# Graph stage: the centre's share in spare rows, layer two's outputs turned by VectorE, and layer one's mapped products in fp32 instead of three bf16 parts

## The chip, the core and the metric

The kernel runs on one core of one Trainium2 chip. Its engines have a queue of instructions each and work beside one another: TensorE (PE, with its weight loads shown apart as PEld), VectorE (DVE), ScalarE (ACT), GpSimd (POOL) and SyncE (SP), which here only starts DMAs. Semaphores tie them together. The metric is device time in microseconds; lower is better. About 0.2% is what a measurement of this kernel can tell from no change.

## What is computed

One layer of a model in three parts: a cross-attention that is a graph convolution over 512 nodes, a state-space scan, and a feed-forward part. The change is in the first. There are 16 batches, 512 nodes each, 32 channels; for each of 4 orders (two Morton, two Hilbert, from the coordinates) a node has K = 10 neighbours, a window of its place in the order.

```python
def _get_graph_features(feats, inds_list, perm, W_lin, b_lin, k=10):
    for inds in inds_list:                       # 4 orders
        neigh = gather(feats, inds)              # (B, N, k, C)
        gf = concat([broadcast(center), neigh - center], -1)
    ...
    x16 = x.astype(float16).astype(float32)      # (B*N, k, 256): 8 heads of 32
    scores = einsum('bihd,bjhd->bhij', qh, qh) / sqrt(32)
    attn = softmax(scores, -1)                   # k x k for each head and node
    out = einsum('bhij,bjhd->bihd', attn, qh).reshape(B * N, k, 256)
    return out @ W_lin.T + b_lin                 # 64 channels

g1 = _get_graph_features(f0, inds_list, perm1, W_lin1, b_lin1)
h1 = lrelu(instance_norm(einsum('oc,bnkc->bonk', W_conv1, g1), (2, 3)))
feats1 = h1.max(-1)                              # 32 channels
g2 = _get_graph_features(feats1, inds_list, perm2, W_lin2, b_lin2)
h2 = lrelu(instance_norm(einsum('oc,bnkc->bonk', W_conv2, g2), (2, 3)))
feats2 = h2.max(-1)                              # 64 channels
h3 = einsum('oc,bcn->bon', W_conv3, concat([feats, feats1, feats2], 1))
return lrelu(instance_norm(h3, (2,)))
```

The centre's half of the heads has the same row ten times, so attention leaves it as it is: its share of an output is a linear map of the node's own features plus the bias, the same for the node's ten rows.

## The kernel before

`graph_part` first makes the sort keys of the nodes (`node_orders`, VectorE, integer operations), then ranks by comparing all keys (L556, L557), then works through eight passes, `order`: four groups of four batches, each through layer one (32 output channels, `co`) and later layer two (64; `npair` is 1 and 2): (0,1), (1,1), (0,2), (2,1), (1,2), (3,1), (2,2), (3,2) as group and layer. The instruction order is written out by hand (`manual_schedule`): each engine gets its instructions in the order of the program. Before the passes GpSimd writes zeros into the tiles that need them (L437), DD and EN last.

A pass is 43 blocks of 12 nodes, 120 (node, neighbour) columns. A block's steps, in the loop at L1090, with how many blocks later each comes:

- `differences` (six blocks ahead): GpSimd subtracts the centre from the window, into DD (f16); every third block four DMAs on SP's queue copy DD into DX, ordered by head.
- `scores` (0): TensorE, a mask matmul (L862) and 16 matmuls (L869) of 120 columns. `greatest` (0): VectorE's maximum (L878). `expo` (1): a matmul subtracts it (L886), ScalarE takes the exponent (L891). `sums` and `shares` (1): VectorE sums (L898) and takes reciprocals (L904), GpSimd multiplies into EN (L906). `turn` (3): VectorE transposes EN in 32x32 blocks (L912) into e.
- `mapped` (0): TensorE takes the differences through the combined weights WA, which are kept as three bf16 parts: 4 x 3 x 4 = 48 matmuls (L931) of 4 `co` columns, each with 32 columns of DD as weights, so that four run beside one another in the array ("128*32"). ScalarE copies the result to `us` (L936).
- `outputs` (3): 16 fp32 matmuls (L959), `us` as weights and e as moving data, 30 columns each; layer one has 32-wide weights, layer two 64-wide ("128*64"). The profile shows each fp32 matmul as two. Columns are output channels' rows: channels lie on partitions. In layer one a matmul with the identity (L949) first writes the centre's share `hc`, repeated ten times, over four blocks' columns. In layer two VectorE adds `hc` (L976).
- `reduce` (4) and `rest` (5): VectorE takes the maximum over the neighbours (L982) and the moments (L985), every four blocks in layer one, every two in layer two.

Beside the blocks run, one piece a block, the preparation of the next pass (`prep`: transposes, one-hot rows by rank L767, placing matmuls L721, DMAs on SP's queue, and `share`, which makes `hc` with L682 and L683), the end of the last pass (`end`, `lrelu_norm`, `finish`) and the rank comparisons that are still wanted. e has 32 rows per block of three nodes, of which 30 are used.

Of the kernel before, what the change touches and what calls it, by code (L numbers as in the profile page):

```python
# [8 lines left out]
F32 = mybir.dt.float32  # L9
# [384 lines left out]
def graph_part(nc, tc, cx, I, dram, id32, ones, xt, F0, layernorm_steps, rstd_steps, scan_input):  # L394
# [43 lines left out]

    layers = []
    for L, co in ((1, 32), (2, 64)):  # L440
        WA = [gc.tile([P, 4, 4, co], BF16, name=f"WA{L}_{k}") for k in range(3)]
        WC = gc.tile([P, co // 32, P], F32, name=f"WC{L}")
        for t in (*WA, WC):
            zero(t)
        layers.append((L, co, co // 32, WA, WC, gc.tile([P, 1], F32, name=f"HB{L}")))

    KS = []
    for k in range(2):
# [14 lines left out]
    nc.vector.memset(W3, 0.0)  # L463
    for b in range(4):
        cols = slice(32 * b, 32 * b + 32)
        for j in range(2):
            nc.sync.dma_start(out=W3[cols, j, cols], in_=I["wc3T"][32 * j:32 * j + 32])
        nc.sync.dma_start(out=W3[64 * (b % 2):64 * (b % 2) + 64, 2 + b // 2, cols], in_=I["wc3T"][64:128])

    it2 = gc.tile([P, D], F16, name="it2")  # L470
    nc.gpsimd.iota(it2, pattern=[[2, D]], base=-(D - 1), channel_multiplier=0, allow_small_or_imprecise_dtypes=True)
# [18 lines left out]
        )  # L490
    for t in (*DD, *EN):
        zero(t)

    idb = gc.tile([P, P], BF16, name="idb")
    nc.scalar.copy(idb, id32)
# [4 lines left out]

    def weights(L, co, npair, WA, WC, HB):
        wa, wc, wt, bl = (loaded[n, L] for n in ("wlA", "wlC", "wcT", "bl"))


        pw = kps.tile([P, 4, co], F32, tag="w", name=f"pw{L}", bufs=2)
        for b in range(4):
            for h in range(4):
                nc.tensor.matmul(
                    pw[32 * b:32 * b + 32, h], lhsT=wa[:, 32 * h:32 * h + 32], rhs=wt, start=(h == 0), stop=True,
                    skip_group_check=True,  # L510
                )

        pc = kps.tile([P, co], F32, tag="w", name=f"pc{L}", bufs=2)
        for b in range(4):
            for m in range(M):
                nc.tensor.matmul(
                    pc[32 * b:32 * b + 32, :], lhsT=wc[:, 32 * m:32 * m + 32], rhs=wt,
                    start=(m == 0), stop=(m == M - 1),
                )
        yield  # L520
        rows = [slice(32 * b, 32 * b + 32) for b in range(4)]
        for k in range(3):
            for b, rb in enumerate(rows):
                nc.scalar.copy(WA[k][rb, :, b], pw[rb])
            if k == 2:
                break
            for b, rb in enumerate(rows):
                nc.tensor.matmul(
                    pw[rb], lhsT=nid[rb, rb], rhs=WA[k][rb, :, b], start=False, stop=True,
                    skip_group_check=True,  # L530
                )
        for b in range(4):
            pr, k = divmod(b * co, P)
            nc.scalar.copy(WC[32 * b:32 * b + 32, pr, k:k + co], pc[32 * b:32 * b + 32, :])

        wt4 = wp.tile([64, P], F32, name=f"wtr{L}")
        nc.scalar.copy(
            wt4.rearrange("p (r o) -> p r o", o=co), wt.unsqueeze(1).to_broadcast([64, P // co, co])
        )
        pb = kps.tile([P, 1], F32, tag="w", name=f"pb{L}", bufs=2)  # L540
        nc.tensor.matmul(pb, lhsT=wt4, rhs=bl, start=True, stop=True)
        nc.scalar.copy(HB, pb)


    sgn = keep.tile([P, D], BF16, name="sgn")
# [97 lines left out]
    def prep(g, layer, early=False):  # L643
# [26 lines left out]
        def share():  # L670

            c16 = wk.tile([P, D], F16, tag="c16", name=f"c16{key}", bufs=1)
            nc.vector.tensor_copy(c16, src)
            yield
            c32 = wk.tile([P, D], F32, tag="c32", name=f"c32{key}", bufs=1)
            nc.vector.tensor_copy(c32, c16)
            yield
            yield
            hc = wk.tile([P, npair, D], F32, tag="hc", name=f"hc{key}")
            for pr in range(npair):  # L680
                ph = ps_1.tile([P, D], F32, tag="misc", bufs=2, name=f"ph{key}_{pr}")
                nc.tensor.matmul(ph, lhsT=WC[:, pr], rhs=c32, start=True, stop=True)  # L682
                nc.scalar.activation(hc[:, pr], ph, AF.Identity, bias=HB)  # L683
                yield
            made[key][2] = hc

        made[key] = [None, None, None]
        if not at_hand:
# [154 lines left out]
    def begin(at):  # L843
        g, layer = order[at]
        L, co, npair, WA, WC, HB = layers[layer]
        key = keys[at]
        per = 4 // npair
        nst = -(-NGRP // per)
        mxo = wk.tile([P, npair, D], F32, tag="mxo", name=f"mxo{key}")
        stats = wk.tile([P, npair, nst, 6], F32, tag="stats", name=f"stats{key}")  # L850
        state[at] = key, co, npair, WA, made[key][2], per, mxo, stats

    def at_piece(at, gi):
# [54 lines left out]
    def turn(at, gi):  # L908
# [3 lines left out]
        nc.vector.transpose(e.rearrange("p i q -> p (i q)"), en.rearrange("p i q -> p (i q)"))  # L912
        live["e2", at, gi] = e

    def mapped(at, gi):

        key, co, npair, WA = state[at][:4]
        slot, c1 = at_piece(at, gi)
        d = DD[slot]
        us = sm.tile([P, NJ, 4 * co], F32, tag="us", name=f"us{at}_{gi}", bufs=4)  # L920
        u = None
        nj = NJ // npair
        for j in range(NJ):
            c0 = c1 + j * QB
            jj = j % nj
            if jj == 0:
                u = ps_2.tile([P, nj, 4 * co], F32, tag="u", name=f"u{at}_{gi}_{j}")
            for k in range(3):
                for h in range(4):
                    rh = slice(32 * h, 32 * h + 32)  # L930
                    nc.tensor.matmul(  # L931
                        u[rh, jj], lhsT=d[:, h, c0:c0 + 32], rhs=WA[k][:, h].rearrange("p b o -> p (b o)"),
                        start=(jj == 0 and k == 0), stop=(k == 2), skip_group_check=True,
                    )
            if jj == nj - 1:
                nc.scalar.copy(us[:, j - jj:j + 1], u)  # L936
        live["us", at, gi] = us

    def outputs(at, gi):
        key, co, npair, WA, hc, per = state[at][:6]  # L940
        us, e = live.pop(("us", at, gi)), live.pop(("e2", at, gi))
        slot = gi % per
        if slot == 0:
            live["h", at] = ps_1.tile([P, npair, per * NQ], F32, tag="h", name=f"h{at}_{gi}")
            if npair == 1:

                f0 = gi * NG
                nn = min(f0 + per * NG, D) - f0
                nc.tensor.matmul(  # L949
                    live["h", at][:, 0, :nn * K].rearrange("p (n j) -> p n j", j=K), lhsT=id32,  # L950
                    rhs=hc[:, 0, f0:f0 + nn].unsqueeze(2).to_broadcast([P, nn, K]), start=True, stop=False,
                    skip_group_check=True,
                )
        h = live["h", at]
        for j in range(NJ):
            for b in range(4):
                pr, r = divmod(b * co, P)
                q0 = slot * NQ + j * QB
                nc.tensor.matmul(  # L959
                    h[r:r + co, pr, q0:q0 + QB], lhsT=us[:, j, b * co:(b + 1) * co],  # L960
                    rhs=e[:, 4 * j + b, :QB], start=npair > 1, stop=True, skip_group_check=True,
                )
        if slot == per - 1 or gi == NGRP - 1:
            live["full", at, gi] = h

    def reduce(at, gi):
        key, co, npair, WA, hc, per, mxo, stats = state[at]
        h = live.pop(("full", at, gi), None)
        if h is None:
            return  # L970
        f0 = (gi - gi % per) * NG
        nn = min((gi + 1) * NG, D) - f0
        hs = h[:, :, :nn * K].rearrange("p r (n j) -> p r n j", j=K)
        if layers[order[at][1]][0] == 2:
            t = sm.tile([P, npair, per * NG, K], F32, tag="hs", name=f"hs{at}_{gi}", bufs=1)
            nc.vector.tensor_tensor(  # L976
                t[:, :, :nn], hs, hc[:, :, f0:f0 + nn].unsqueeze(3).to_broadcast([P, npair, nn, K]), ALU.add,
            )
            hs = t[:, :, :nn]

        def greatest_of():
            nc.vector.tensor_reduce(mxo[:, :, f0:f0 + nn], hs, AX.X, ALU.max)  # L982

        def moments(pr):
            nc.vector.bn_stats(stats[:, pr, gi // per], hs[:, pr].rearrange("p n j -> p (n j)"))  # L985

        if npair == 1:
            greatest_of()
            moments(0)
        else:  # L990
            moments(0)
            live["rest", at] = lambda: (greatest_of(), moments(1))
        if gi == NGRP - 1:
# [7 lines left out]
    def end(at):  # L1001

        g, layer = order[at]
        key, co, npair, WA, hc, per, mxo, stats = state.pop(at)
        res = []
        for pr in range(npair):
            mv = sm.tile([P, 2], F32, tag="mv", name=f"mv{key}_{pr}")
# [1 line left out]
            r = sm.tile([P, 1], F32, tag="hr", name=f"hr{key}_{pr}")  # L1009
            yield from rstd_steps(sm, r, mv[:, 1:2], 1, f"h{key}_{pr}")  # L1010
            dst = F1[g] if layer == 0 else wk.tile([P, D], F32, tag=f"F2_{pr}", name=f"F2_{key}_{pr}", bufs=1)
            yield from lrelu_norm(dst, mxo[:, pr], mv[:, 0:1], r, f"{key}_{pr}")
            res.append(dst)
        if layer == 1:
            yield from finish(g, res)

    def lrelu_norm(dst, src, mean, r, key):
        t = wk.tile([P, D], F32, tag="lr", name=f"lr{key}", bufs=1)
        nc.vector.tensor_scalar(t, src, mean, r, ALU.subtract, ALU.mult)
        yield  # L1020
        nc.vector.scalar_tensor_tensor(dst, t, 0.2, t, ALU.mult, ALU.max)
        yield
# [64 lines left out]

    ahead = {}
    blocks = [(at, gi) for at in range(len(order)) for gi in range(NGRP)]
    for it in range(len(blocks) + 5):  # L1090

        def do(step, lag):
# [15 lines left out]
            rank_step(later_tile)  # L1108
        do(greatest, 0)
        do(mapped, 0)  # L1110
        do(sums, 1)
        if at + 1 == len(order) and gi == 4:
            tails.extend(scan_input(sm, junk(q), q) for q in range(NBG - 1))
# [705 lines left out]
```

## Time and profile before

| | |
|---|---|
| median of 3 runs | 2256.55 us (2255.29 to 2256.65) |
| profiled execution | 2259.84 us, span 2258.1 us, granted clock 0.978 |
| TensorE busy | 2058.6 us (91%), 40533 matmuls |
| weight loads | 1272.5 us (56%), 40586 |
| VectorE busy | 1792.6 us (79%) |
| ScalarE busy | 1132.6 us (50%) |
| GpSimd busy | 833.6 us (37%) |
| L931, all layers | 412.7 us, 16512 matmuls |
| L959, 128*64 (layer two) | 194.3 us, 5504 |
| L959, 128*32 (layer one) | 83.8 us, 5504 |
| L949 | 45.8 us, 88 |
| L976 | 53.3 us, 84 recorded |

Busy time is the union of an engine's instructions; ends of matmuls are modelled, so that a busy TensorE is not TensorE at its peak. In groups and timelines a line holds the code line, the engine, the operation, out<-in by the program's names, partitions x elements and types, and the count; brackets show how long the engine had been idle and what ended it, where "issue" means that the profile shows nothing that it waited for. A duration is longer than the distance to the next start of the same engine where instructions overlap; distances between starts are used for what an instruction costs. A few matmul records can be missing. The passes begin, by the first L862 of each, at 94.8, 253.6, 393.9, 547.0, 694.7, 847.2, 991.0 and 1143.7 us; the last block starts before 1291.5.

### The profile page before, as it was taken

The page shows a single profiled execution, that of the slowest core. Times are in us where ns is not written, and L with a number is a line of the kernel's source. Part 1 is how long each engine was busy: PE and PEld are TensorE (multiplying, and loading weights), DVE is VectorE, ACT ScalarE, POOL GpSimd, SP SyncE. Part 2 cuts the span into 40 slices and gives each one's busy share as a digit, 9 for nine tenths or more (in the row PEclk, how much of TensorE's full clock was granted, in tenths as well). Part 3 has the DMA queues.
Part 4 walks back from the last instruction along what each step waited for, and adds up shares of the span by engine and source line. Part 5 has one row for each costly group of instructions (what it writes and reads, how often), then busy time and mean ns, then how long its engine had stood idle before and what let it go on. Part 6 is the DMA issues. An engine that isn't in the chain of part 4 may idle for free. (4 is left out here: it accounts for less than half of the span.)

```text
span 2258.1 us, 91857 instructions
## 1 busy us (share of the span) xinstructions
PE 2058.6 (91%) x40533; PEld 1272.5 (56%) x40586; DVE 1792.6 (79%) x3972; ACT 1132.6 (50%) x2066; POOL 833.6 (37%) x913
## 2 busy tenths in 40 slices
PE   5599898999888998889999969988999999999998
PEld 2255555777456775567777734445465564656443
DVE  8488797999988999989999964397968668685554
ACT  5686577556666554445555523343545445353521
POOL 2156656556556565565555400021112111020210
PEclk9899999999999999999999979999999999999999
DMA  1323233142242321422311122211221312113210
GB/s 45 78 65 79 53 74 73 42 87 49 52 88 47 75 61 41 90 50 62 74 36 43 31 63 61 85 58 44 86 75 38 103 47 75 66 47 94 52 38 19
DMA packets 126395, 138.25 MB, mean 61 GB/s; under 512 B 21051, under 2 KB 84261, under 8 KB 125997
## 3 DMA queue, kind: packets, MB, share of 16 engines
q1 hardware_dynamic: 125997, 132.37, 23.1%
q8 instruction: 319, 5.23, 1.0%
q14 instruction: 79, 0.65, 0.1%
HBM read 77.02 MB, written 12.85 MB: 40 GB/s over the span
## 5 line engine op out<-in xcount | busy, mean ns | idle before, releaser
L906 POOL TENSOR_TENSOR EN<-e,rz 128x480 f32<-128x480 f32 x344 | 342.5, 996 | 500.8 <-DVE rz L904 415.1
L931 PE MATMUL u<-WA,DD 128*32 128x128 bf16 (+1 forms) x16512 | 412.7, 247 | 29.1 <-issue 28.3
L936 ACT COPY us<-u 128x512 f32<-128x512 f32 x516 | 302.1, 587 | 153.3 <-PE u L931 137.8
L931 PEld LDWEIGHTS <-DD 128*32 128x32 f16 x16512 | 337.7, 97 | 52.5 <-issue 50.9
L891 ACT ACTIVATE e<-s,smc 128x480 f32<-128x480 f32 x344 | 227.7, 662 | 255.3 <-PE s L886 222.9
L827 POOL TENSOR_TENSOR DD<-fs,crep 128x480 f16<-128x480 f32 (+2 forms) x344 | 349.7, 1017 | 0.0
L959 PEld LDWEIGHTS h<-e,us 128*32 128x32 f32 (+1 forms) x11008 | 244.9, 125 | 136.0 <-issue 68.9
L959 PE MATMUL h<-e,us 128*32 128x30 f32 (+1 forms) x11008 | 278.1, 210 | 32.8 <-issue 15.0
L1393 POOL TENSOR_TENSOR ssq<-ssq,sq 128x512 f32<-128x512 f32 x56 | 79.5, 1419 | 580.4 <-ACT sq L1392 580.4
L878 DVE TENSOR_REDUCE c<-s 128x16 bf16<-128x480 f32 x344 | 220.6, 641 | 85.2 <-PE s L869 81.5
L1200 PE MATMUL ppg<-hT,wing 128*128 128x512 f32 x512 | 239.9, 612 | 0.0
L1213 DVE SCALAR_TENSOR_TENSOR cyh<-ppch,t_conv_w,cyh 128x496 f32<-128x496 f32 (+2 forms) x192 | 137.5, 716 | 119.8 <-ACT cyh L1207 115.3
L1200 PE MATMUL ppch<-hT,winch 128*128 128x512 f32 x512 | 230.9, 593 | 0.7 <-ACT gs L1288 0.7
L912 DVE STREAM_TRANSPOSE e<-EN 128x512 f32<-128x512 f32 x344 | 224.7, 653 | 0.0
L898 DVE TENSOR_REDUCE z<-e 128x16 f32<-128x480 f32 x344 | 219.6, 638 | 0.4 <-ACT e L891 0.4
L557 ACT ACTIVATE sgn<-kd 128x512 bf16<-128x512 f32 x256 | 153.1, 598 | 50.2 <-PE kd L556 35.0
L869 PEld LDWEIGHTS <-DD 128*32 128x32 f16 x5504 | 80.7, 96 | 157.5 <-issue 134.3
L767 DVE TENSOR_SCALAR oh<-it,rank 128x512 bf16<-128x512 f16 x512 | 156.4, 366 | 9.3 <-PE pp L721 9.3
L869 PE MATMUL s<-DX,DD 128*32 128x120 f16 x5504 | 141.8, 221 | 19.0 <-DMA DX<-DD 14.6
L1200 PEld LDWEIGHTS ppch<-hT,winch 128*128 128x128 f32 x512 | 94.3, 190 | 110.8 <-issue 102.1
L1200 PEld LDWEIGHTS ppg<-hT,wing 128*128 128x128 f32 x512 | 95.1, 193 | 102.6 <-issue 98.9
L886 PE MATMUL s<-c,idb 128*128 128x480 bf16 x344 | 130.0, 378 | 6.0 <-DVE c L878 2.7
(368 smaller groups left out, 2991.2 us busy)
## 6 DMA issues: line engine op xcount, KB each, us to landing
DX<-DD SPq DMA_DIRECT2D x456, 90.0 KB
wing<-in_in_proj SPq DMA_DIRECT2D x64, 256.0 KB
winch<-in_in_proj SPq DMA_DIRECT2D x64, 256.0 KB
wo<-in_out_proj SPq DMA_DIRECT2D x64, 256.0 KB
crep<-dC SPq DMA_DIRECT2D x128, 64.0 KB
dS<-so SPq DMA_DIRECT2D x32, 256.0 KB
fs<-dS SPq DMA_DIRECT2D x128, 64.0 KB
wincB<-in_in_proj SPq DMA_DIRECT2D x8, 256.0 KB
```

Of the source, the lines that this page charges most:

```text
L767: nc.vector.tensor_scalar(oh[:, j], it2, rank[:, c, m, 4 * g + b:4 * g + b + 1], None, ALU.is_equal)
L827: nc.gpsimd.tensor_tensor(d[:, :, m0 - n0:n1 - n0], win, crep[:, :, m0:n1].unsqueeze(3).to_broadcast([P, 4, n1 - m0, K]), ALU.subtract,)
L869: nc.tensor.matmul(s[rh, j * 4 * QB:(j + 1) * 4 * QB].rearrange("p (b q) -> p b q", b=4), lhsT=d[:, h, c0:c0 + 32], rhs=dx[:, h, :, c0:c0 ...
L878: nc.vector.tensor_reduce(c, live["s", at, gi].rearrange("p (i q) -> p i q", q=QB), AX.X, ALU.max, negate=True)
L891: nc.scalar.activation(e, s.rearrange("p (i q) -> p i q", q=QB), AF.Exp, scale=smc)
L898: nc.vector.tensor_reduce(z, e, AX.X, ALU.add)
L906: nc.gpsimd.tensor_tensor(en[:, :, :QB], e, rz.unsqueeze(2).to_broadcast([P, NI, QB]), ALU.mult)
L912: nc.vector.transpose(e.rearrange("p i q -> p (i q)"), en.rearrange("p i q -> p (i q)"))
L931: nc.tensor.matmul(u[rh, jj], lhsT=d[:, h, c0:c0 + 32], rhs=WA[k][:, h].rearrange("p b o -> p (b o)"), start=(jj == 0 and k == 0), stop=(k ...
L936: nc.scalar.copy(us[:, j - jj:j + 1], u)
L959: nc.tensor.matmul(h[r:r + co, pr, q0:q0 + QB], lhsT=us[:, j, b * co:(b + 1) * co], rhs=e[:, 4 * j + b, :QB], start=npair > 1, stop=True, ...
L1200: nc.tensor.matmul(pp, lhsT=w[:, k], rhs=hT[:, k], start=(k == 0), stop=(k == 3))
```

## The change

Layer one's WA is one fp32 tile instead of three bf16 parts. As both operands of a matmul are then fp32, a new step `widen` has ScalarE copy a block's DD into an fp32 tile, one block ahead. `share` computes the centre's share with the bias for all nodes, nodes on partitions, and stores it to DRAM (`hT`). A new step `centres`, one block after `mapped`, has SP load the three times four nodes' rows into row 30 of each 32 rows of `us`; EN's column 30 holds, from the start on, a one for the node that a row belongs to (`own_node`), so that the outputs' matmuls add the centre's share by themselves. L949 and L976 go. Layer two's outputs have e as weights (32 wide) and `us` as moving data (64 columns), so that they come out with rows on partitions, and VectorE turns them with a 32x32 transpose out of PSUM before the maximum and the moments. The layout of `mxo` and `stats` follows, and so W3's rows and `lrelu_norm`, which takes two instructions instead of one.

```diff
-        WA = [gc.tile([P, 4, 4, co], BF16, name=f"WA{L}_{k}") for k in range(3)]
+        WA = [gc.tile([P, 4, 4, co], dt, name=f"WA{L}_{k}") for k, dt in enumerate(((F32,), (BF16,) * 3)[L - 1])]
...
-        for j in range(2):
+        for j in range(4):
             nc.sync.dma_start(out=W3[cols, j, cols], in_=I["wc3T"][32 * j:32 * j + 32])
-        nc.sync.dma_start(out=W3[64 * (b % 2):64 * (b % 2) + 64, 2 + b // 2, cols], in_=I["wc3T"][64:128])
...
     for t in (*DD, *EN):
         zero(t)
+    own_node = kp.tile([P, NB], F32, name="own_node")
+    nc.gpsimd.memset(own_node, 1.0)
+    for base, cm, step in ((0, 1, -32 - K), (K - 1, -1, 32 + K)):
+        nc.gpsimd.affine_select(out=own_node, in_=own_node, ...)
+    for en in EN:
+        nc.vector.tensor_reduce(en[:, 0, QB:QB + 1], own_node, AX.X, ALU.add)
+        nc.vector.tensor_copy(en[:, 1:, QB:QB + 1], en[:, 0:1, QB:QB + 1].to_broadcast([P, NI - 1, 1]))
...
-            for pr in range(npair):
-                ph = ps_1.tile([P, D], F32, tag="misc", bufs=2, name=f"ph{key}_{pr}")
-                nc.tensor.matmul(ph, lhsT=WC[:, pr], rhs=c32, start=True, stop=True)
-                nc.scalar.activation(hc[:, pr], ph, AF.Identity, bias=HB)
+            hT = dram.tile([D, 4 * co], F32, name=f"hT{key}")
+            nch = 4 // npair
+            for c0 in range(0, 4, nch):
+                ph = ps_1.tile([P, nch, 4 * co], F32, tag="misc", bufs=2, name=f"ph{key}_{c0}")
+                nc.tensor.matmul(ph, lhsT=id32, rhs=HB.unsqueeze(1).to_broadcast([P, nch, 4 * co]), ...)
+                for c in range(nch):
+                    nc.tensor.matmul(ph[:, c], lhsT=c32[:, (c0 + c) * P:(c0 + c + 1) * P], rhs=WC..., ...)
+                nc.scalar.copy(hc, ph)
                 yield
+                nc.sync.dma_start(out=hT[c0 * P:(c0 + nch) * P].rearrange("(c p) o -> p c o", p=P), in_=hc)
...
+    def widen(at, gi):
+        if order[at][1]:
+            return
+        slot, c1 = at_piece(at, gi)
+        d = wk.tile([P, 4, NQ + 2], F32, tag="d32", name=f"d32{at}_{gi}", bufs=2)
+        nc.scalar.copy(d, DD[slot][:, :, c1:c1 + NQ + 2])
...
-            for k in range(3):
+            for k in range(len(WA)):
...
+    def centres(at, gi):
+        hT = state[at][4]
+        us = live["us", at, gi]
+        f0 = gi * NG
+        whole = min(NG, D - f0) // NB
+        left = min(NG, D - f0) - whole * NB
+        at_30 = us[QB:QB + 32 * (NB - 1) + 1:32]
+        nc.sync.dma_start(out=at_30[:, :whole], in_=hT[f0:f0 + whole * NB].rearrange("(j n) o -> n j o", n=NB))
+        ...
     def outputs(at, gi):
-                nc.tensor.matmul(
-                    live["h", at][:, 0, :nn * K].rearrange("p (n j) -> p n j", j=K), lhsT=id32,
-                    rhs=hc[:, 0, f0:f0 + nn].unsqueeze(2).to_broadcast([P, nn, K]), start=True, stop=False, ...)
...
+                else:
+                    nc.tensor.matmul(
+                        hv[rb, :, slot, j], lhsT=e[:, 4 * j + b],
+                        rhs=us[:, j, b * co:(b + 1) * co].rearrange("p (c o) -> p c o", c=2), ...)
...
     def reduce(at, gi):
-            nc.vector.tensor_tensor(
-                t[:, :, :nn], hs, hc[:, :, f0:f0 + nn].unsqueeze(3).to_broadcast([P, npair, nn, K]), ALU.add)
...
+            ht = sm.tile([P, 2, 2 * NJ, 32], F32, tag="ht", name=f"ht{at}_{gi}", bufs=1)
+            nc.vector.transpose(ht.rearrange("p c x q -> p (c x q)"), h)
...
     def lrelu_norm(dst, mxo, pr, n, mean, r, key):
-        nc.vector.tensor_scalar(t, src, mean, r, ALU.subtract, ALU.mult)
+        nc.vector.tensor_scalar(t[:, :full * n]..., mxo[:, :full, of], mean, r, ALU.subtract, ALU.mult)
+        nc.vector.tensor_scalar(t[:, full * n:], mxo[:, full, ...], mean, r, ALU.subtract, ALU.mult)
...
+    widen(*blocks[0])
     for it in range(len(blocks) + 5):
...
         do(mapped, 0)
+        do(centres, 1)
+        do(widen, -1)
         do(sums, 1)
```

## The prediction

> **What bounds the kernel now.** Four views, in this order: the table of stretches, cut at the first mask matmul (L862) of each of the eight passes; TensorE's timeline inside a layer-one pass; TensorE's and VectorE's inside a layer-two pass; the first 55 us. The scan and the last part, behind 1291 us, are not touched. First a layer-one and a layer-two pass (43 blocks each; PE, PEld, DVE, ACT, POOL, clock, DMA):
>
> ```profile
> 253.60:393.90 140.30, 125.48 (x4478) 75.90 (x4500) 122.28 (x274) 100.41 (x224) 85.65 (x95) 1.00 0.32 70
> 393.90:547.00 153.10, 149.34 (x4416) 114.27 (x4414) 144.33 (x343) 83.29 (x140) 87.24 (x96) 1.00 0.28 61
> ```
>
> A layer-two block takes 3.56 us and TensorE is busy for 98% of it, VectorE for 94%. A layer-one block takes 3.26 us and no engine is above 90%. Both hold about 209 TensorE instructions, loads and matmuls together ((4478 + 4500) / 43). Where layer one's time goes, TensorE's timeline says:
>
> ```profile
> 956.20 0.68 PE L931 MATMUL u<-WA,DD 128*32 128x128 bf16 x33 [0.74 <-issue]
> 956.96 1.04 PE L949 MATMUL h<-hc,id 128*128 128x480 f32 x2
> 957.93 0.46 PE L959 MATMUL h<-e,us 128*32 128x30 f32 x32
> 958.32 0.38 PE L886 MATMUL s<-c,idb 128*128 128x480 bf16 x1
> 958.53 0.37 PE L862 MATMUL s<-mR,mL 128*128 128x480 bf16 x1
> 958.83 0.41 PE L869 MATMUL s<-DX,DD 128*32 128x120 f16 x16
> 959.06 0.78 PE L931 MATMUL u<-WA,DD 128*32 128x128 bf16 x42
> 960.82 0.29 PE L931 MATMUL u<-WA,DD 128*32 128x128 bf16 x6 [0.98 <-issue]
> ...
> 962.69 0.36 PE L959 MATMUL h<-e,us 128*32 128x30 f32 x24
> 964.84 0.27 PE L959 MATMUL h<-e,us 128*32 128x30 f32 x8 [1.78 <-issue]
> ```
>
> TensorE stops in the middle of a run, waiting for no semaphore. From 956.20 to the stop before 960.82 there are 33+2+32+1+1+16+42 = 127 matmuls, with their loads 254 instructions; to the next stop again about 256. The page has 319 instruction packets in 5.23 MB, 16 KB each: 256 instructions of 64 bytes, for 81,119 on TensorE. I read the stops as TensorE running out of fetched instructions. They come every 3.7 to 4.6 us in such stretches: 256 per 4.1 us, 62 per us, and 209 of them give 3.35 us a block, which is what this pass (847 to 991) takes. Breaks over 0.3 us inside runs, added from the timeline, come to some 14, 8, 8 and 15 us in the four layer-one passes, and 4 us in all of layer two.
>
> ```profile
> 1181.21 1.48 PE L931 MATMUL u<-WA,DD 128*32 128x256 bf16 x48
> 1182.62 1.12 PE L959 MATMUL h<-e,us 128*64 128x30 f32 x32
> 1183.68 0.38 PE L886 MATMUL s<-c,idb 128*128 128x480 bf16 x1
> ...
> 1259.92 0.65 DVE L912 STREAM_TRANSPOSE e<-EN 128x512 f32<-128x512 f32 x1
> 1262.89 0.65 DVE L912 STREAM_TRANSPOSE e<-EN 128x512 f32<-128x512 f32 x1
> 1265.70 0.65 DVE L912 STREAM_TRANSPOSE e<-EN 128x512 f32<-128x512 f32 x1
> ```
>
> In layer two TensorE has no gap: 3.21 us a block, 1.06 of it the outputs (L959). VectorE is close behind. Where it catches up without a gap it does two blocks in 5.78 us, 2.89 each; blocks that also make one-hots (L767, four of 0.27 us) cost it 3.81 against TensorE's 3.85.
>
> ```profile
> 2.94 0.68 DVE L217 TENSOR_REDUCE mn<-X 48x1 f32<-48x512 f32 x1 [0.28 <-DMA X<-in_coords]
> 13.37 1.09 POOL L437 MEMSET EN<- 128x512 f32 x2
> 51.67 1.04 PE L296 MATMUL prh<-id,KH 128*32 128x128 f32 x4 [4.26 <-DVE KH L281]
> ```
>
> At the start the sort keys are one chain on VectorE, from 2.94 us until TensorE, idle, gets KH at 51.67. The first pass starts behind it.
>
> **The change part by part,** on the profiled execution: 2259.84 us, of which 2258.1 are the span. The median of the runs is 3.3 lower.
>
> *Start.* VectorE's sums of `own_node` into EN stand ahead of the keys, and they wait for GpSimd, whose queue ends with EN's zeros at 14.46. Layer one's single fp32 WA saves it 0.33 us of zeros; three small operations add some 0.6 (0.23 each, as L816). Four small ones on VectorE add 0.7, so the keys begin at 15.4 instead of 2.94: 12.5 later. Without the neighbour both engines speed up: L482 on GpSimd took 1.37 us while VectorE worked, its twin L487 0.78; VectorE's L244 took 1.27, its like L243 0.68, and L237 1.28. I give back 2: +10.4. In the first `share` a bias matmul of 512 fp32 columns joins one that took 2.05 us; ScalarE's ranks queue behind it: +1.7. Together +12 (8 to 15). Nothing covers it: the chain runs through VectorE.
>
> *Layer one's products.* 48 bf16 matmuls of 128 columns take 0.67 us to the next group (962.02 to 962.69). An fp32 matmul shows as two (32 in L959 for 16), so 32 of 128 columns replace them, 4096 columns. The nearest row is 8 x 512 = 4096 fp32 columns on the same 128*32 tiles:
>
> ```profile
> 2222.24 1.06 PE L1743 MATMUL fpa<-fg,fa2r 128*32 128x512 f32 x8
> ```
>
> Less the 0.18 us of tail that L931 also shows (0.85 against 0.67), 0.88: +0.21 x 172 blocks = +36. The centre matmul (L949, 956.96 to 957.93, 0.97) goes 44 times: -43. Net -7 of TensorE, half of it on the path: -3 (-10 to +8).
>
> *Layer one's instructions.* A block loses 32 of 209, and L949's: 176. At 62 per us that is 2.85 us, no more than TensorE's own work (about 2.8 us a block without the breaks). The 45 us of breaks should fall by two thirds, 30, and two thirds of that is on the path, since VectorE is the late one elsewhere: -20 (-40 to 0). [...]
>
> *`widen`.* 172 ScalarE copies of 488 columns, as L936's 0.59: 101 us. The idle 40 us of a layer-one pass hide them. One loop is new: products, `us` copy, `widen`, next products: 0.88 + 0.2 + two copies at 0.55 + 0.1 = 2.3 us, above the fastest blocks now (1.8 to 2.2): +4 (0 to +12).
>
> *Layer two's outputs.* 32 matmuls on 32-wide tiles instead of 64-wide. Layer one's 32 of 30 columns take 0.39 us (957.93 to 958.32); 2048 columns at L1743's rate 0.44 to 0.53. I take 0.53 against 1.06; staying in one tile shape saves 0.10 more (1.41 from L931 to L959 here, 1.31 where a group of the same shape follows). TensorE falls to 2.58 a block, so VectorE's 2.89 decides: 0.32 at most. There are 16 blocks of 3.2 us in each of three passes, 15 us; the 18 one-hot blocks of each give 0.03, 1.5; the last pass, with the finishing work on VectorE (idle 7.0 there), gives 3: 19.5. But 206 instructions at 2.9 us are 256 in 3.6, just under the shortest spacing of the stops, and I take a third off: -13 (-25 to 0).
>
> *The turn.* 88 transposes from PSUM replace the additions (84 recorded, 0.65 to the next start). L912 from SBUF needs 0.57. For PSUM, L878 (641 ns) against L898 from SBUF (638, same shape) says no difference: 0.66, +1 (-5 to +6). [...]
>
> *Small.* Twelve more `tensor_scalar` at 0.16 in the ends: +2. Bias matmuls of later shares, beside VectorE's F3 splits: +1. `centres`: 344 transfers and 4 for remainders of at most 12 rows on SP's queue; ten-row loads (L550) cost 0.33 us of issue, so SP, a third busy, carries them. Issued one block behind the products, they are wanted two blocks later: +1.5 (0 to +60, see the first rival). What waits with them is TensorE, and with it the next exponents and scores.
>
> Sum: 12 - 3 - 20 + 4 - 13 + 1 + 2 + 1 + 1.5 = -14.5: 2245.3, less 3.3: 2242.
>
> **Rivals.**
> (1) Slower: the spare rows arrive late. SP is in order, and DX's four issues in every third block wait for GpSimd's DD and then take 2.4 us (3.66 seen at 1185.59), so `centres` can leave 5.9 us after a block's start, with 7.1 to go before its outputs. If issue to landing passes about 2 us in all those 115 blocks, each waits some 0.5: +57, 2299. Against: L550's loads have no waits of note in the passes.
> (2) The fetch stays the limit: breaks shrink only with the instructions (16% of 45, -7), layer two gains nothing because 62 per us already is its 3.2 us, and the start still costs 12: +12 - 3 - 7 + 4 + 5.5 = +11.5, 2268. For: layer two's rate equals the starved one. Against: it shows no breaks.
> (3) Everything on TensorE counts: breaks gone (-35), layer two down to VectorE's floor (-25): -41, 2215.
> (4) The fp32 products do not run four wide: 32 x 0.109 = 3.5 us a block, +2.6 x 172 = +450. L1743 speaks against it.
>
> **How the numbers follow.** Forecast 0.56, its own range 2226 to 2258; rivals 0.14, 0.12, 0.16, 0.02. About 0.2% (4.5 us) is what can be told from no change. Faster: 0.46 of the forecast and all of (3): 0.62. The same: 0.09 of the forecast, 0.02 of (2): 0.11. Slower: the rest, 0.27. The range 2214 to 2274 leaves out half of (3), nearly all of (1), and (4).
>
> **What would show it.** VectorE's first reduction of X near 15 us and the first pass near 107; L931's fp32 form 0.88 us to the next group; mid-run stops few in layer-one passes; the layer-two outputs at 0.5 us and blocks near 3.0 with VectorE nearly gapless. I am wrong if TensorE waits for a DMA into `us`, if stops appear in layer two, or if `widen` ends waits of the products.

## The result, and the profile after

The changed kernel is slower: 2273.99 us against 2256.6, a ratio of 1.0071 (95% interval 1.0045 to 1.0097). A second set of runs, on another chip, gave 1.0091 (1.0059 to 1.0122). Its profiled execution took 2277.95 us, 18.1 more than the one of before (2259.84). I had forecast 2242 us. Most of what I took for the substance of the change happened at about the forecast size; two things that the new transfers do to SP's queue ate it up.

Cut at the first mask matmul (now L884) of each pass, the two profiled executions compare like this (us; sums over the four passes of each layer):

| | first pass starts | layer-one passes | layer-two passes | behind the passes | span |
|---|---|---|---|---|---|
| before | 94.8 | 590.6 | 606.1 | 966.6 | 2258.1 |
| after | 113.6 | 603.7 | 594.0 | 964.9 | 2276.2 |
| difference | +18.8 | +13.1 | -12.1 | -1.7 | +18.1 |
| forecast | +12 | -17.5 | -12 | +3 | -14.5 |

(The forecast by its terms: the start; products, fetch, widening and `centres`; outputs and turn; and the small rest, whose place it did not split.) The start lost 7 us more than forecast, layer two gained what was forecast, and layer one lost 13 where it should have gained 17.5. The second and third passes in the table of stretches, with the columns of the one of before:

```profile
278.30:423.00 144.70, 133.44 (x3799) 82.91 (x3798) 124.22 (x277) 115.78 (x267) 86.39 (x95) 0.98 0.33 73
423.00:571.00 148.00, 132.33 (x4422) 98.60 (x4420) 143.13 (x342) 83.26 (x141) 86.44 (x96) 0.99 0.30 68
```

Layer two is as forecast: TensorE fell from 149 us to 132 and VectorE is busy for 97% of the pass. Layer one sends 15% fewer matmuls (3799 against 4478) and yet takes 4.4 us longer. What TensorE waits for there is in the list of its waits (us in total, times, longest), first of after, then of before:

```profile
PE s L908 <- DVE c L900: 36.4, 84, 0.8
PE h L1002 <- DMA us<-hT: 30.7, 21, 3.9
...
PE kd L565 <- DMA kr<-others: 11.9, 1, 11.9
...
PE h L1002 <- issue: 8.9, 9, 1.9
...
PE h L1007 <- DMA us<-hT: 8.2, 9, 2.2
...
PE u L964 <- issue: 3.2, 8, 0.9
```
```profile
PE u L931 <- issue: 28.3, 66, 2.2
PE h L959 <- issue: 15.0, 13, 4.2
```

The mid-run stops ("issue") have shrunk: over the eight passes, all such gaps of TensorE come to 22.9 us instead of 50.4. That is 11.7 instead of 47.8 in layer one; in layer two they have grown from 2.7 to 11.2. In place of layer one's stand waits for the centre's rows, `us<-hT`, 39 us in all, 30.7 of them in the outputs of layer one (L1002), and one wait of 11.9 us for keys at the start. The 36.4 us for `c` (L900), almost all of them in layer two, are layer two's new limit: TensorE now waits for VectorE.

The longest wait for the rows, on TensorE and then on SP:

```profile
401.74 1.08 PE L964 MATMUL u<-WA,d 128*32 128x128 f32 x32
402.76 0.39 PE L565 MATMUL kd<-kr,kl 128*128 128x512 bf16 x1
407.08 0.65 PE L1002 MATMUL h<-e,us 128*32 128x30 f32 x32 [3.93 <-DMA us<-hT]
```
```profile
396.06 0.72 SPq L980 DMA_DIRECT2D us<-hT  x1
397.56 3.08 SPq L859 DMA_DIRECT2D DX<-DD  x4
400.68 0.52 SPq L559 DMA_DIRECT2D kr<-others  x1
401.25 0.34 SPq L560 DMA_DIRECT2D kl<-own  x1
...
404.11 0.33 SPq L559 DMA_DIRECT2D kr<-others  x1
404.48 0.33 SPq L560 DMA_DIRECT2D kl<-own  x1
404.91 2.38 SPq L980 DMA_DIRECT2D us<-hT  x3
```

SP issues nothing for the rows from 396.8 to 404.9. First come the four DX loads of the next piece, then the eight loads of the next comparison keys. Three blocks' rows then go out one after the other, and TensorE resumes 2.2 us after the first of them was issued. How long the DX loads hold the queue over the eight passes while they wait for GpSimd's DD is in the list of SP's own waits:

```profile
SPq L859 <- POOL DD L849: 347.9, 109, 7.5
```

The rows, 352 issues (the prediction had counted 348) of some 0.72 us, also keep SP itself busier: the time that it is issuing DMAs in the passes rises from 459 to 731 us, from 38% to 61%.

The start, on VectorE and on SP:

```profile
12.93 0.16 DVE L502 TENSOR_REDUCE EN<-own_node 128x1 f32<-128x3 f32 x1 [10.27 <-POOL own_node L497]
...
13.47 0.67 DVE L217 TENSOR_REDUCE mn<-X 48x1 f32<-48x512 f32 x1
```
```profile
72.25 0.38 SPq L560 DMA_DIRECT2D kl<-own  x1
77.79 0.40 SPq L704 DMA_DIRECT2D hT<-hc  x1
78.29 9.95 SPq L719 DMA_DIRECT2D crep<-dC  x16
88.88 0.28 SPq L559 DMA_DIRECT2D kr<-others  x1
```

The chain of the keys starts at 13.47 instead of 2.94 us, as forecast. What I had not seen is the second fence. SP stands still from 72.6 to 77.8 because the next thing in its queue is the store of `hT`, and ScalarE has not made `hc` yet. Behind the store are 16 loads of `crep`, and behind these the keys that TensorE then waits 11.9 us for. In the kernel before, the `crep` loads were issued from 64.48 to 71.83 and the keys at 72.24, 16.6 us earlier.

### The profile page after: what moved, and what is told of

Read it like the earlier page. It is cut to its first block, busy times and chain, and to the rows that moved or that the text cites. A ratio compares the mean times of both kernels' runs of the same rounds, so it can differ in the third digit from the quotient of the medians.

```text
span 2276.2 us, 87880 instructions
## 1 busy us (share of the span) xinstructions
PE 2001.3 (88%) x37802; PEld 1226.0 (54%) x37802; DVE 1798.4 (79%) x4004; ACT 1201.3 (53%) x2230; POOL 831.9 (37%) x914
## 5 line engine op out<-in xcount | busy, mean ns | idle before, releaser
L969 ACT COPY us<-u 128x512 f32<-128x512 f32 x516 | 302.3, 587 | 173.3 <-PE u L964 160.8
L900 DVE TENSOR_REDUCE c<-s 128x16 bf16<-128x480 f32 x344 | 219.8, 639 | 75.8 <-PE s L891 75.1
L964 PE MATMUL u<-WA,DD 128*32 128x256 bf16 x8256 | 263.1, 275 | 3.2 <-issue 2.7
L964 PEld LDWEIGHTS <-DD 128*32 128x32 f16 x8256 | 215.5, 98 | 10.9 <-issue 7.1
L964 PE MATMUL u<-WA,d 128*32 128x128 f32 x5504 | 191.7, 280 | 2.8 <-ACT e L913 1.4
L891 PEld LDWEIGHTS <-DD 128*32 128x32 f16 x5504 | 81.0, 96 | 158.9 <-issue 131.9
L964 PEld LDWEIGHTS u<-WA,d 128*32 128x32 f32 x5504 | 145.1, 112 | 34.8 <-issue 11.6
L908 PE MATMUL s<-c,idb 128*128 128x480 bf16 x344 | 129.6, 377 | 38.6 <-DVE c L900 36.4
L891 PE MATMUL s<-DX,DD 128*32 128x120 f16 x5504 | 141.9, 222 | 18.2 <-DMA DX<-DD 14.6
L1277 PEld LDWEIGHTS ppg<-hT,wing 128*128 128x128 f32 x512 | 93.8, 191 | 100.9 <-issue 97.3
```

The costliest lines, as they stand in the source:

```text
L891: nc.tensor.matmul(s[rh, j * 4 * QB:(j + 1) * 4 * QB].rearrange("p (b q) -> p b q", b=4), lhsT=d[:, h, c0:c0 + 32], rhs=dx[:, h, :, c0:c0 ...
L900: nc.vector.tensor_reduce(c, live["s", at, gi].rearrange("p (i q) -> p i q", q=QB), AX.X, ALU.max, negate=True)
L964: nc.tensor.matmul(u[rh, jj], lhsT=d[:, h, c0:c0 + 32], rhs=WA[k][:, h].rearrange("p b o -> p (b o)"), start=(jj == 0 and k == 0), stop=(k ...
L1277: nc.tensor.matmul(pp, lhsT=w[:, k], rhs=hT[:, k], start=(k == 0), stop=(k == 3))
```

## The experiments

Theory Q: in layer one the loss is the place of the row loads in SP's queue, and the gain of the fp32 products lies hidden beneath it. Theory S: the start loses 8.3 us to `own_node` and 10.5 to the place of `hT`'s store. The rivals were that the new work itself (fp32 products, widening copies) is what costs, and that the transfers are slow wherever they stand. All kernels below were timed in five rounds beside the kernel before; ratios are to that. The runs of one kernel scatter by 5 to 20 us, so a profiled execution can lie several us off its kernel's median, and single stretches are compared only where the difference is larger than that of kernels run twice. Passes and starts are from the profiled executions.

| run | median us | ratio (95%) | first pass starts | layer one | layer two | waits for rows | mid-run stops |
|---|---|---|---|---|---|---|---|
| after, again | 2276.9 | 1.0091 (1.0059-1.0122) | 114.3 | 602.6 | 595.8 | 32.7 | 30.2 |
| e1 no rows | 2243.6 | 0.9958 (0.9946-0.9971) | 112.2 | 573.6 | 590.3 | 0 | 20.6 |
| e2 own_node late | 2268.3 | 1.0060 (1.0041-1.0079) | 105.5 | 597.5 | 589.2 | 33.2 | 16.8 |
| e3 store by ScalarE | 2273.2 | 1.0077 (1.0052-1.0103) | 107.9 | 598.8 | 591.3 | 30.1 | 27.0 |
| e4 three bf16 parts | 2283.6 | 1.0142 (1.0124-1.0161) | 112.8 | 603.2 | 598.0 | 18.5 | 78.7 |
| e5 rows early | 2264.4 | 1.0033 (1.0017-1.0049) | 114.0 | 582.0 | 590.4 | 6.8 | 31.1 |
| e6 all moved | 2242.1 | 0.9942 (0.9920-0.9964) | 97.3 | 586.4 | 591.5 | 10.5 | 36.1 |
| e6 again | 2241.9 | 0.9946 (0.9928-0.9965) | 99.4 | 585.4 | 591.7 | 13.7 | 25.5 |
| e7 moved, bf16 | 2259.5 | 1.0020 (1.0005-1.0034) | 97.0 | 598.2 | 600.0 | 8.4 | 96.7 |
| e8 keys spread | 2234.7 | 0.9908 (0.9885-0.9930) | 95.4 | 584.1 | 592.8 | 10.9 | 31.7 |
| e8 again | 2235.7 | 0.9893 (0.9870-0.9917) | 94.5 | 583.7 | 591.4 | 10.4 | 30.4 |
| e9 moved, no rows | 2229.6 | 0.9891 (0.9871-0.9911) | 97.0 | 577.7 | 587.7 | 0 | 17.5 |

**The changed kernel without the row loads (e1).**

```diff
-        do(centres, 1)
```


> The changed kernel with the loads of the centre's rows into us left out, so the centre's share is missing from its output; hT is still made and stored. Theory Q (SP's queue): in the changed kernel TensorE waits some 33 us in the four layer-one passes and 8 us in layer two for these loads, which stand behind DX's and the keys' loads on SP. Without them most of that is regained: the layer-one passes take about 572 us together (604 with them, 591 in the kernel before) and the whole about 2238 us (2230 to 2248). Rival W (work): fp32 products and the widening copies make the layer-one loop longer and the waits only fill slack; then other waits take their place, the layer-one passes stay near 600 us and the whole above 2262 us.

Layer one takes 573.6 us, 30 less than in the profile of after and 17 less than before; layer two another 3.7 less. The ratio falls by 0.011 to 0.013, 25 to 30 us. So the rows cost what theory Q said, and the rival that other waits would take the place of these falls; that it is their place in the queue is for e5 to show. The 17 us that layer one is now under the kernel before, although its first pass starts 17 us late, are what I had forecast for products, fetch and widening together (19).

**The `own_node` operations behind the keys (e2).** The four VectorE operations are put behind the last key load of the start.

```diff
-    for en in EN:
-        nc.vector.tensor_reduce(en[:, 0, QB:QB + 1], own_node, AX.X, ALU.add)
...
     load_keys(0, (2, 3))
+    for en in EN:
+        nc.vector.tensor_reduce(en[:, 0, QB:QB + 1], own_node, AX.X, ALU.add)
```


> The changed kernel with VectorE's four own_node operations put behind the sort keys instead of ahead of them. Theory S (start): they hold the keys' chain behind GpSimd's zeros; KH comes at TensorE near 51.7 us instead of 59.96, the first pass starts 8 us earlier (105.5 instead of 113.6) and the whole takes about 2266 us. Rival: the first pass waits for hT's store and the key loads behind it anyway, so that nothing is gained (2274 us).

KH reaches TensorE at 51.36 us and the first pass starts at 105.5, both as expected. The wait for the keys behind the `hT` store stays (11.6 us), so the two losses add up rather than cover each other. By the time alone this run can't be told from the changed kernel: the ratio is 0.001 to 0.003 lower, with intervals that overlap; 8 us would be 0.0036.

**`hT`'s store from ScalarE's queue (e3).**

```diff
-                nc.sync.dma_start(
+                nc.scalar.dma_start(
                     out=hT[c0 * P:(c0 + nch) * P].rearrange("(c p) o -> p c o", p=P), in_=hc
```


> The changed kernel with hT's store issued from ScalarE's queue instead of SP's. Theory S: in the first share the store holds SP until ScalarE has copied hc, and with it the 16 loads of crep and the next keys; without it the keys that TensorE waits 11.95 us for come some 9 to 11 us earlier, the first pass starts near 103.5 instead of 113.6 and the whole takes about 2264 us. Rival: the 16 crep loads alone make the keys late and the store only adds its 0.4 us of issue; then 2273 us.

The first pass starts 5.7 us earlier, not 10, and the time shows nothing. The timeline of SP says why:

```profile
72.20 0.33 SPq L560 DMA_DIRECT2D kl<-own  x1
72.63 11.47 SPq L719 DMA_DIRECT2D crep<-dC  x16
84.20 0.28 SPq L559 DMA_DIRECT2D kr<-others  x1
```

SP no longer stands still, but the 16 `crep` loads now take 11.47 us to issue instead of 7.35. Nine of them go out by 76.12, but the tenth only at 81.77, and the trace names the landing of `hT`'s store, which ScalarE issued at 78.71, as what released it. So the store still holds up the loads, now from another queue. It does so by a shared wait and not by its traffic: in the traces of the changed kernel and of this one the program's 1632 DMAs take eight semaphores in turn, 204 each, and an issue first waits until the DMA that had its semaphore before has landed: in after the ninth `crep` load goes out at 81.67 us, 0.02 us behind the landing of the first. The tenth load has the semaphore of the store. What the store needs is a later moment, not another queue. Theory S had only the first half.

**Three bf16 parts again (e4),** with the spare rows as in the change: the WA tiles are bf16 and the `widen` calls are gone.

```diff
-        WA = [gc.tile([P, 4, 4, co], dt, name=f"WA{L}_{k}") for k, dt in enumerate(((F32,), (BF16,) * 3)[L - 1])]
+        WA = [gc.tile([P, 4, 4, co], dt, name=f"WA{L}_{k}") for k, dt in enumerate(((BF16,) * 3, (BF16,) * 3)[L - 1])]
...
-        do(widen, -1)
```


> The changed kernel with layer one's products as three bf16 parts again, and so without the widening copies; the centre's share stays in the spare rows. Theory Q: the rows' waits stay (some 30 us in layer one), TensorE's products get 0.2 us a block shorter, but 16 more instructions a block bring the mid-run stops of the kernel before back; the two overlap in part: 2266 to 2284 us, layer-one passes 596 to 614 us. Rival W: the fp32 products and the copies are what costs; then the layer-one passes fall to 575 us and the whole to about 2245 us.

Layer one stays at 603.2 us, so fp32 is not what costs. But its make-up changes: waits for the rows fall to 18.5 us and mid-run stops rise to 78.7. Each hides part of the other. (With their loads the added instructions are 32 a block, not 16.) By the ratio it is slower than the changed kernel (1.0142 against 1.0071 and 1.0091).

**The changed kernel again,** as the measure for the next three.

> The changed kernel unaltered, as the measure for the three beside it on the same chip. Every theory: 1.007 times the kernel before, 2270 to 2274 us, with TensorE's waits for the rows in us near 40 us in all.

It came out at 1.0091, with 32.7 us of waits for the rows.

**The rows asked for earlier (e5).** Only the place of the calls changes: ahead of the same iteration's `differences`, which issues DX's loads.

```diff
-        do(centres, 1)
...
+        do(centres, 0)
         if it + LEAD < len(blocks):
             to, g2 = blocks[it + LEAD]
```


> The changed kernel with one thing moved: a block's centre rows are asked for at the end of the same iteration, ahead of the next DX loads on SP, and not one iteration later behind them. Theory Q: the waits come from the place in the queue; they fall from 40 us to under 12, the layer-one passes to 575 to 585 us together and the whole to 2240 to 2250 us. Rival D (transfer): the rows are late because the transfer itself is slow or the queue is full; then the waits stay above 25 us and the whole above 2262 us.

The waits for the rows fall to 6.8 us with the same bytes on the same queue, and layer one to 582.0: where the loads stand in the queue was the cause, and rival D falls. The move puts them ahead of the DX loads and asks for them earlier; this run doesn't part the two. Both shorten the same stretch: from a block's products standing in `us` to the issue of its rows, the median in layer one is 5.0 us in after and 2.3 here. The transfer itself is not slow, as rival D had it: in the longest wait of after TensorE resumed 2.2 us behind the issue. The time fell by 0.6% (1.0091 to 1.0033), 13 us, about half of what I had expected; why not more is open. This profiled execution is the fastest of its twelve runs (2255.5 against a median of 2264.4), so its stretches flatter the kernel.

**The start mended as well (e6).** The `own_node` operations as in e2, and the first `hT` store held back until the start's loads are issued:

```diff
+                if early:
+                    held.append(store_h)
+                else:
+                    store_h()
...
     load_keys(4, range(M))
+    for store_h in held:
+        store_h()
```


> As the kernel with the rows asked for early, with the start mended too: VectorE's own_node operations behind the sort keys, and the first hT's store behind the first crep and key loads on SP. Theory S: the first pass starts near 96 us instead of 113.6 (94.8 in the kernel before), 16 to 18 us less than with the rows alone: 2222 to 2234 us, which is 1.0 to 1.5% under the kernel before. Rival: the start shifts only part of the way (103 us or later), and the whole stays above 2238 us.

> The kernel with rows and start moved once more, as the measure for the two beside it: 0.994 times the kernel before, 2238 to 2246 us, some 8 us of waits for the rows left.

The first pass starts at 97.3 and 99.4 us, 16.7 and 14.6 earlier than in e5. The whole is at 0.9942 and 0.9946, 22 us under e5 and with it a kernel that computes everything is for the first time clearly under the kernel before. That is some 5 to 8 us more than the start's 15 to 17, and where these come from is open. Both sides of the start are shown: 18.8 us were lost, and putting two things later brings 15 to 17 back. `own_node` accounts for 8.1 of them by e2, the store for the other 6 to 8; the 2.5 and 4.6 us that are left over the kernel before are open.

**Rows and start moved, with three bf16 parts (e7).**

> As the kernel with rows and start moved, but with layer one's products as three bf16 parts and without the widening copies. Theory F (instruction fetch): with no row waits to hide them the mid-run stops cost their full price, some 50 to 60 us of TensorE idle without a releaser, and the kernel is 12 to 25 us slower than with fp32 products: 2238 to 2255 us. Rival W: fp32 products take TensorE 0.2 us a block longer and the copies lengthen the loop, so three bf16 parts are as fast or faster: 2225 us or less.

This is the plain test of the fetch reading: two kernels that differ only in how layer one's products are made. With bf16 it is 17.5 us slower (0.78%), though each block's products take TensorE 0.2 us less (0.67 us in the kernel before against 0.87 in after) and ScalarE has no widening copies to make. The gaps that TensorE's list of waits puts down to "issue", first of e6 (fp32; the products are L969, layer one's outputs L1007), then of e7 (bf16; L967 and L1005):

```profile
PE h L1007 <- issue: 15.4, 14, 2.6
...
PE u L969 <- issue: 10.1, 28, 0.9
```
```profile
PE u L967 <- issue: 42.4, 85, 1.8
...
PE h L1005 <- issue: 28.0, 34, 2.3
```

All mid-run stops of the passes come to 36.1 us against 96.7. The granted clock is not the reason: the second set of e6 took 2240 to 2244 us at 0.972 to 0.982, e7 2255 to 2267 at 0.973 to 0.980. In the profiled executions 11.8 us of the loss lie in layer one and 8.5 in layer two, whose own instructions are the same in both; why layer two takes part is open.

Where the stops stand says that they are waits for instructions. Counted over all of TensorE's instructions, the stops of more than 0.3 us are a multiple of 256 instructions apart, within 10, in 39 of 41 cases in the kernel before and in 90 of 97 in e7; chance would give 8%. TensorE resumes a median of 1.43 us after the end of the last packet of the queue that carries instructions, in both (1.2 to 1.6 us in eight of ten cases). In none of the fourteen traces do two such packets (16 KB each) start less than 3.23 us apart (3.31 in the kernel before, 3.30 in after), and 256 instructions per 3.23 us are 79 per us. Why e7 stops for longer than the kernel before (50.4 us), which issues about as many instructions (319 instruction packets to 320), is open.

**The key loads spread (e8).** Of the waits for the rows that are left in e6, the longest (3.0 us) stands behind this on SP:

```profile
632.00 1.24 SPq L864 DMA_DIRECT2D DX<-DD  x2
633.28 0.52 SPq L555 DMA_DIRECT2D kr<-others  x1
...
637.24 0.32 SPq L556 DMA_DIRECT2D kl<-own  x1
637.61 1.62 SPq L768 DMA_DIRECT2D fs<-dS  x4
639.33 2.37 SPq L985 DMA_DIRECT2D us<-hT  x3
```

so the burst of eight loads was taken apart:

```diff
-        elif k == 4 and b + 1 < B:
-            load_keys(b + 1, range(M))
+        elif k in (4, 6, 8, 10) and b + 1 < B:
+            load_keys(b + 1, (k // 2 - 2,))
```


> The kernel with rows and start moved, and the eight loads of the next comparison keys, which come in one burst on SP, spread over four steps of two. Theory Q: what waits for the rows are left (7.9 us) stand behind that burst; they fall below 4 us, the layer-one passes from 586 to about 580 us and the whole by 4 to 6 us to 2234 to 2240 us. Rival: the burst hides; no change, 2242 us, or slower where the spread loads get in the way of others.

> The kernel with the key loads spread, once more: its first profile still held 10.9 us of waits for the rows, as without the spreading, though its median was 7 us lower. If the spreading works by those waits, this profile shows them under 5 us and the time is again 0.990 to 0.992 times the kernel before. If the gain was scatter between runs, the ratio comes back to 0.994 and the waits stay near 10 us.

The time fell twice, to 0.9908 and 0.9893, 6 to 7 us under e6 in the medians. The reason I gave did not show: the waits for the rows are 10.9 and 10.4 us in all, as in e6. They moved: in layer one they are 6.3 and 5.8 us instead of 8.9 and 10.8, in layer two 4.7 and 4.6 instead of 1.7 and 2.8. The first pass starts 2 to 5 us earlier and layer one is 1 to 3 us shorter, little more than two profiles of one kernel differ; where the rest comes from is open. It is the fastest of the kernels that compute everything: 2235 us, 0.9 to 1.1% under the kernel before.

**What the rows still cost (e9):** e6 without the row loads.

> The kernel with rows and start moved, but with the loads of the centre's rows left out, so the centre's share is missing from its output: what the rows still cost. Theory Q: little is left to gain, 8 to 14 us (2228 to 2234 us), with layer-one passes near 574 us as in the first run without rows. Rival: the row loads are free now, 2240 us or more.

2229.6 us, 12 under e6. So the rows are still not free there, but their price went from about 30 us (e1 against after) to 12.

## Why the prediction was wrong

**The step that failed** is `centres`, priced at +1.5 (0 to +60). I argued that SP, a third busy, carries the loads and that they are wanted two blocks later. Their lateness came not from the queue's share but from what stood ahead of them when they became ready. e1 puts the price at 34 us in the two profiles (30.1 in layer one, 3.7 in layer two), and e5 shows that it lies in where the loads stand in the queue. My own rival 1 named the mechanism, SP in order and the rows behind DX's loads, and I gave it 0.14. I argued against it with the key loads (L550), which nobody waited for: but those are asked for long before they are needed, and as a burst of eight they are part of what the rows stand behind. I also took 0.33 us for one issue, from these loads; the row loads take 0.72. And I worked the risk out on a block of layer two; it struck mainly in layer one, in three of whose four passes the key loads run too.

**The start** was the second miss: +12 forecast, +18.8 measured. Of the two parts, `own_node` was right in kind and a little large (+10.4 against 8.3: the zeros were done earlier than I took them, so the chain began 10.5 us later, and quicker VectorE operations gave back 2.2: L237 took 0.54 us instead of 1.28, L244 0.68 instead of 1.27). The other 10.5 us are not the bias matmul (+1.7 forecast; the first one-hot products, at 79.40 us, are 7.3 later than before, less than KH's 8.3). Most of them, 6 to 8 us by e6, are the store of `hT`, a DMA that I did not follow past `crep` and the keys on SP; the rest is open.

**Right** were the terms that carried the forecast. Layer one's fp32 products take 0.87 us to the next group (956.95 to 957.82), 0.88 forecast. Layer one's mid-run stops fell from 47.8 us to 11.7 and 16.1 in after's two profiles and 7.4 in e1, by the two thirds that I had said or more. In layer two they grew from 2.7 us to 11 to 14, which I had named as a sign of being wrong; for that risk I had taken a third off. All of layer one without the rows: -17 against -19, and with the rows moved the fp32 products are worth 17.5 us (e7 against e6), 11.8 of them in layer one. The outputs of layer two take 0.55 to 0.62 us (0.53 forecast), and where TensorE runs freely a block takes 2.60 (2.58 forecast):

```profile
1203.61 0.62 PE L1007 MATMUL h<-us,e 128*32 128x64 f32 x32
1204.16 0.38 PE L908 MATMUL s<-c,idb 128*128 128x480 bf16 x1
...
1206.21 0.62 PE L1007 MATMUL h<-us,e 128*32 128x64 f32 x32
```

The passes of layer two gained 12.1 us, with VectorE busy for 94 to 97% of each, as forecast. That the size fits is partly luck: without the rows the gain is 15.8 (e1), and waits for rows took part of it away. The turn from PSUM takes 0.67 us, as taken from the row of L878; it costs 0.70 to the next start, where the addition had 0.65.

**Rival 2** (fetch as a limit of 62 instructions per us) falls: layer two runs three blocks like the one above in a row, from 1200.97 to 1208.81 us, without a stop: 196 matmuls and loads a block in 2.61 us, 75 per us. What I took for a rate in the kernel before was the mean of work and stops. The spacing of the instruction packets, never under 3.23 us, suggests a limit all the same, at 79 per us by my estimate, and layer one's work before, by the prediction's account 209 instructions in about 2.8 us (75 per us on the average), came close to it.

Corrected in these two terms alone, the sum -14.5 + 6.8 + 32.5 comes to +24.8, against +18.1 measured. The 6.7 us between the two are layer two, which without the rows gained 3.8 us more than forecast, and the time behind the passes, where 1.7 were gained instead of 3 lost, less the 2 us that layer one without the rows stayed short of its forecast.

## What to carry to other kernels

A new load is priced by listing what stands ahead of it on its queue at the moment it becomes ready: the waits of those, and the bursts. The queue's busy share did not tell that here: SP was issuing for 38% of the passes before, 61% after, and TensorE waited 39 us for the rows, up to 3.9 at once. A change that removes work can lose by where its new DMAs stand, and here the same DMAs and four small VectorE operations, a few places up or down the program, turned +0.7 to +0.9% into -0.6%. Follow every store of a preparation step through the queue as well, above all at the start, where nothing else fills the time.

## What the runs showed of the hardware that I had not expected

- The 16 `crep` loads of 64 KB took 7.35 us to issue alone, 9.95 right behind the 256 KB store of `hT` and 11.47 with that store issued from another queue in their midst. In the first two cases the first eight or nine went out 0.35 us apart, the rest 0.6 and 0.9 us apart: from there on each waits for the landing of the load eight before it, as the program's DMAs share eight semaphores.
- With bf16 products, TensorE's mid-run stops came to 78.7 and 96.7 us in two kernels that issue as many instructions as the kernel before with its 50.4. Stops are not a fixed price per 256 instructions, though they stand at multiples of 256; what sets their length was not found.
